# An attention and expert-FFN kernel on one core: the order of the first loads, a load issued from ScalarE's queue, and a planner that holds less urgent steps back

## The chip, the cores and the metric

The kernel runs on one core of a Trainium2 chip. A core has TensorE (PE, the matmuls, with its weight loads listed apart as PEld), VectorE (DVE), ScalarE (ACT), GpSimd (POOL) and SyncE (SP), which issues most of the DMA transfers. Each engine works through its own list of instructions in order and waits on semaphores for the others. The time is the device time of one launch in microseconds (us); before the change the median of three runs is 1022.4 us (1019.82 to 1022.9).

## The reference

x has 8 sequences of 1024 tokens with 256 features. A normalized attention without softmax over tokens, and a gated sum over 16 experts, each with a layer norm behind it:

```python
qkv = x @ Wqkv + bqkv;  q, k, v = split(qkv)          # each 256 wide
q = q - mean(q);  k = k - mean(k)
q2 = q*q / (sum(q*q) + eps);  q2 = q2 / norm of q2 along features
k2 = k*k / (sum(k*k) + eps);  k2 = k2 / norm of k2 along the tokens
kv = k2^T v;  t2 = q2 kv / sqrt(1024)                  # per sequence
x = layernorm(x + (v + t2) @ Wln + bln)
sel = sigmoid(x . expert_sel)                          # 16 gates per token
out = sum over e of sel_e * relu(x @ keys_e) @ values_e   # 256 -> 128 -> 256
x = layernorm(x + out)
```

## The kernel before, in words

Tokens are cut into 16 chunks of 512 (`NCHK`, two to a sequence). A matmul's operands are split into a high and a low part of fp32r type (`xh`/`xl` and so on), and three products are added (`passes3`, line 52). `nh`/`nl` are the same tokens with the tokens on the partitions, from x; `xh`/`xl` have the features there, from xT.

For each chunk c: `tokens_x` and `tokens_n` load and split x; `u_k` projects K (`kp`), squares it (`k`, sums in `ks`), scales it, splits it (`k2h`, `k2l`) and multiplies it with x's rows (`ap`, summed over a sequence in `asb`); `u_m` makes a matrix per sequence from it (`mc`, `pm`, `mh`, `ml`); `u_q` projects Q (`qp`), normalizes it (`qs`, `qj`, `qn`, `qy`) and turns it (`qt`, `q2h`, `q2l`); `u_y` makes the first layer norm's input (`yp`; `ych`, `ycl`, squares `ysq`) and the gates. For chunk 0 the gates go through `gates_first` (line 782): `tt`, `zt`, small steps on `gv`, `gy`, `zs`, `za`, a turn `gt`, a copy `gs`, and matmuls `gsp` that spread the first three gates over the partitions (`selb`). Then come 16 experts: `h` (or, for half of the pairs from chunk 1 on, `hx` and `hy` with fewer products), gating, the split `sh`/`sl`, and the second product into `w`. `u_end` normalizes and stores. `u_weights` loads and splits the experts' weights in four groups (`kst`, `keyh`, `keyl`; `vst`, `vst_m`, `valh`, `vall`). At the start K's weights (`sk`), Q's (`sq`), the output weights (`sl`) and V's (`svT`), a row of biases (`brow`) and small columns (`bc`, `eft`) are loaded; `brow` less its mean becomes `bhl` (lines 1231 to 1242), which is added to K and Q of chunks 0 and 1 by a matmul with `rows`.

No instruction stands where the code names it. `add` only records a task: its engine or engines, a cost, a key and what it reads and writes. `order` (line 202) then simulates all engines with these costs and writes the instructions out in the order in which its simulation starts them; a lower key goes first among the ready ones. Tiles share slots by tag (`SB_SLOTS`, `PS_SLOTS`); a task starts only when there is a slot for each new tile. Two features matter here:

- The first three second products of chunk 0 are goals (line 1125). Tasks on which a goal depends have a `tail`, the time from their start to the goal; they are the urgent ones. `sharpen` (line 183) simulates these alone with `pack`, 24 rounds forward and backward, and takes the start times of the best round as keys. All others have no tail, and their keys are the given ones.
- As long as an urgent task is left (`first`) and PE has nothing to start, `order` puts in a filler, `keep_warm` (line 433): two 128 by 128 matmuls into the tile `warm`, which show as four in the trace, with a planned 0.44 us. The number of fillers is fixed when the program is written, so PE runs them all, however fast they go.

The simulation's DMA (lines 285 to 290) gives a load 0.5 us of SP's queue, and then the transfers one behind the other. ACT's first instruction is the load of its function table (line 419).

```python
265  if e == "T" and self.idle and issued and first and now > 0.4:
266      fill = Task()
267      fill.eng, fill.fn, fill.news, fill.start, fill.done = e, {e: self.idle}, [], now, now + 0.44
```

Of the kernel before, what the change touches and what calls it, by code (L numbers as in the profile page):

```python
# [15 lines left out]
P = 128  # L16
# [10 lines left out]
WARM = 14  # L27
WINDOW = 10.47
# [69 lines left out]
class Task:  # L98
    __slots__ = ("eng", "cost", "key", "fn", "port", "deps", "outs", "bufs", "news", "start", "done", "n", "id", "tail")


class Work:
# [5 lines left out]
    def __init__(self, slots):  # L108
        self.slots, self.tasks, self.bufs, self.goals, self.idle = slots, [], [], {}, None
# [6 lines left out]
    def add(self, eng, cost, key, fn, r=(), w=(), port=False, after=()):  # L116

        t = Task()
        if len(eng) == 1:
            cost, fn, port = {eng: cost}, {eng: fn}, {eng: port}  # L120
        t.eng, t.cost, t.key, t.fn, t.port = eng, cost, key, fn, port
        t.id, t.deps, t.outs, t.bufs, t.news = len(self.tasks), set(after), [], {}, []
        for many, writes in ((r, False), (w, True)):
            for x in many:
                b, part = x if isinstance(x, tuple) else (x, None)
                for other, opart, owrites in b.accesses:
                    if (writes or owrites) and meet(part, opart) and other is not t:
                        t.deps.add(other)
                b.accesses.append((t, part, writes))
                t.bufs[b] = None  # L130
        for d in t.deps:
            d.outs.append(t)
        self.tasks.append(t)
        return t

    def pack(self, part, before, rank, release):
# [11 lines left out]
        while len(start) < len(part):  # L148
            now = heapq.heappop(events)
            moved = True  # L150
            while moved:
                moved = False
                for e in free:
# [20 lines left out]
                    end[t] = free[e] + (2.2 if e == "D" else 0.2 if e == "T" else self.LATENCY)  # L174
# [8 lines left out]
    def sharpen(self, rounds=24):  # L183

        part = [t for t in self.tasks if t.tail is not None]
        inside = set(part)
        deps = {t: [d for d in t.deps if d in inside] for t in part}
        outs = {t: [o for o in t.outs if o in inside] for t in part}
        late = max(-x for x in self.goals.values())
        release = {t: late + x for t, x in self.goals.items()}  # L190
        rank, best = {t: t.tail for t in part}, None
        for _ in range(rounds):
            start = self.pack(part, deps, rank, {})
            span = max(start[t] + x for t, x in self.goals.items())
            if best is None or span < best[0]:
                best = span, start
            back = self.pack(part, outs, start, release)
            rank = {t: back[t] + min(t.cost.values()) for t in part}
        for t in part:
            t.key = best[1][t] - 2000  # L200

    def order(self):
# [24 lines left out]
        while left:  # L227
# [7 lines left out]
            while moved:  # L235
# [5 lines left out]
                for e in free:  # L241
# [3 lines left out]
                    for entry in ready[e]:  # L245
# [7 lines left out]
                        if e == "G" and first and t.tail is None and t.port[e]:  # L253
                            continue
                        if e == "G" and t.port[e] and any(o.eng == "V" and o.port["V"] and k < key and w < now + 0.5 for k, _, o, w in ready["V"]):
                            continue
# [7 lines left out]
                    if best is None:  # L264
                        if e == "T" and self.idle and issued and first and now > 0.4:
                            fill = Task()
                            fill.eng, fill.fn, fill.news, fill.start, fill.done = e, {e: self.idle}, [], now, now + 0.44
                            fill.cost, fill.key, fill.bufs, fill.tail = {e: 0.44}, 0, {}, None
                            issued.append(fill)
                            free[e] = now + 0.44  # L270
                            heapq.heappush(events, free[e])
                        continue
# [12 lines left out]
                    if e == "D":  # L285
                        free[e] = now + 0.5
                        dma = max(dma, now + 1.3) + t.cost[e]
                        t.done = max(dma + 0.7, now + 2.2)
# [8 lines left out]
                    t.done += self.LATENCY  # L297
# [25 lines left out]
def attn_ffn_kernel(ctx, tc, x, xT, wqT, wk, wvT, wlnT, bcols, brows, selT, keys, values, outT):  # L323
# [55 lines left out]
    def high(key, h, b, n, r, w, free=True):  # L379

        if free:
            add("VS", {"V": c_dve(n, fast=True), "S": c_act(n, plain=True)}, key,
                {"V": lambda: V.tensor_copy(h(), b()), "S": lambda: S.copy(h(), b())}, r=r, w=w, port={"V": True, "S": False})
        else:
            add("S", c_act(n, plain=True), key, lambda: S.copy(h(), b()), r=r, w=w)
# [33 lines left out]
    S.preload_act_table_set("natural_log_exp_and_others")  # L419

# [16 lines left out]
    add("T", 0.44, -800, keep_warm, r=[ones], w=[warm])  # L437
    work.idle = keep_warm


    def stage(key, src, name, tag="sh"):
        b = sbuf(tag, [P, 2, D], name)
        add("D", 1.05, key, lambda: nc.sync.dma_start(out=b.ap, in_=src), w=[b])
        return b
# [51 lines left out]
    xh, xl, nh, nl = {}, {}, {}, {}  # L496
# [5 lines left out]
    def tokens_x(c, key):  # L502
        xh[c], xl[c] = h, l = [sbuf(t, [P, 2, CH], f"{t}{c}", FR) for t in ("xh", "xl")]
        if c == 0:
            b = sbuf("g3", [P, 2, CH], f"xf{c}")
            for i in range(2):
                w = slice(i * CH // 2, (i + 1) * CH // 2)
                add("D", 1.05, key, lambda w=w: nc.sync.dma_start(out=b[:, :, w], in_=xTv[:, :, w]), w=[(b, i)])
# [8 lines left out]
    def split(c, key, name, src, h, l, width):  # L517

        rows = h.shape[1]
        n = 1 if c < 2 else 2  # L520
        for i in range(n):
# [3 lines left out]
            add("D", 2.1 / n, key, lambda b=b, s=s: nc.sync.dma_start(out=b.ap, in_=src(s)), w=[b])  # L525
            high(key + 1.2, lambda s=s: h[:, s], lambda b=b: b.ap, 2 * CH // n, [b], [(h, part)], c < 2)
# [16 lines left out]
    def project(c, g, t, wh, wl, bias=None):  # L543
        for j in range(2):
# [4 lines left out]
            if bias is not None:  # L549
                terms += [(rows[:, bias, :], bhl[:, 0])]  # L550
            mm_group(t[:, j * D : (j + 1) * D], terms)
# [16 lines left out]
    def u_k(c, key):  # L568
# [7 lines left out]
        for g in range(2):  # L576
            tt = slice(2 * g, 2 * g + 2)
            t = psum(f"kp{c}_{g}", "h" if c == 0 else "att")
            if c < 2:
                add("T", c_mm(D, 14), key + g, lambda g=g, t=t: project(c, g, t, wkh, wkl, 1),  # L580
                    r=x_parts(c, g) + [wkh, wkl, rows, bhl], w=[t])
                squares(key + g + 0.7, q, g, s, t)
                continue
# [6 lines left out]
        for g in range(2):  # L590
# [3 lines left out]
            high(key + 3.5 + g * 0.3, lambda tt=tt: h[:, tt, :], lambda tt=tt: q[:, tt, :], CH, [(q, tt)], [(h, g)], c < 2)  # L594
# [109 lines left out]
    def u_q(c, key):  # L704
# [3 lines left out]
        for g in range(2):  # L708
            tt = slice(2 * g, 2 * g + 2)
            t = psum(f"qp{c}_{g}", "h" if c == 0 else "att")  # L710
            if c < 2:
                add("T", c_mm(D, 14), key + g, lambda g=g, t=t: project(c, g, t, wqh, wql, 0),
                    r=x_parts(c, g) + [wqh, wql, rows, bhl], w=[t])
                squares(key + g + 0.7, q, g, s, t)
                continue
# [34 lines left out]
        for ct in range(2):  # L750
# [6 lines left out]
            add("T", c_mm(P, 4), key + 6.5 + ct * 0.2, turn, r=[q, ident], w=[o])  # L757
# [457 lines left out]
    tokens_x(1, -110)  # L1215
    add("D", 0.1, -198, lambda: nc.sync.dma_start(out=bc.ap, in_=bcols), w=[bc])
# [10 lines left out]
    brow, mb = sbuf("sl", [P, 1, D], "brow"), tiny("brow_m")  # L1227
    bhl, rows0, rows = cbuf("bhl", [P, 1, D], FR), sbuf("t2", [P, 2, P], "rows0"), cbuf("rows", [P, 2, P], FR)
    add("D", 0.15, -197, lambda: nc.sync.dma_start(out=brow[:, 0], in_=brows), w=[brow])
# [123 lines left out]
    with tc.manual_schedule():  # L1353
        for t in work.order():
# [35 lines left out]
```

## Time and profile before

| | us |
|---|---|
| runs | 1019.82, 1022.4, 1022.9 (median 1022.4) |
| the profiled execution's own time | 1020.05 |
| its span, first to last instruction | 1018.3 |
| PE busy | 1008.1 (99%) |
| DVE busy | 784.8 (77%) |
| ACT busy | 667.1 (66%) |
| POOL busy | 470.5 (46%) |
| first K matmul of chunk 0 starts | 9.18 |
| first second product `w` starts | 63.96 |

A line of the profile has start and length in us, the engine, the line of the kernel, the operation, and the output and inputs by the program's names without numbers; "x12" is a number of instructions, and brackets hold the idle time of the engine before the instruction and what ended it. The chain of waits is followed back from the last instruction; the pieces of it lie end to end. A table by stretches has for each stretch the busy time of PE, PEld, DVE, ACT and POOL with the number of instructions, then the mean share of full speed at which TensorE's clock ran, the DMA engines' busy share, and GB/s.

### The profile page before, as it was taken

Reading aid. Unit: us, or ns where it says so; the run is one execution under the profiler, and the core shown is the slowest. Engines: PE = TensorE matmul, PEld = TensorE weight load, DVE = VectorE, ACT = ScalarE, POOL = GpSimd, SP = SyncE. Lnnn points to the kernel's source line nnn. Section 1 sums busy time; section 2 is a strip of 40 time slices with the busy share of each in tenths; the row PEclk is TensorE's granted clock in tenths of the full one; section 3 lists DMA queues with packets and bytes.
Section 4 is the critical chain, followed back from the end, with each engine's and each line's share of the span. In section 5 each row is a group of like instructions: output and inputs, shape, how many; then the busy total and the mean of one; then the engine's idle time right before and its main releaser. Section 6 shows DMA issues by size and latency. Waiting matters only on the chain.

```text
span 1018.3 us, 16317 instructions
## 1 busy us (share of the span) xinstructions
PE 1008.1 (99%) x5757; PEld 874.3 (86%) x5757; DVE 784.8 (77%) x1363; ACT 667.1 (66%) x1497; POOL 470.5 (46%) x424
## 2 busy tenths in 40 slices
PE   9999999999999999999999999999999999999996
PEld 9978879888898988889888888988889888888885
DVE  7889888687776887768787687867878687686775
ACT  7767566675676757766676676757666675665543
POOL 1001585546564464655536574454654536233430
PEclk9999999999999999999999999999999999999999
DMA  6144323233232323323223231323323222223131
GB/s 202 44 135 125 116 94 125 93 90 101 82 121 68 115 94 104 93 89 103 93 89 108 87 115 63 115 94 103 105 71 109 93 85 83 83 85 104 64 125 42
DMA packets 65298, 99.52 MB, mean 98 GB/s; under 512 B 6336, under 2 KB 24896, under 8 KB 65216
## 3 DMA queue, kind: packets, MB, share of 16 engines
q1 hardware_dynamic: 65216, 98.48, 30.1%
q8 instruction: 45, 0.74, 0.3%
q14 instruction: 37, 0.30, 0.1%
HBM read 89.54 MB, written 8.91 MB: 97 GB/s over the span
## 4 chain that ended last, share of the span: by engine, by line
PE 93%; DVE 3%; POOL 2%; ACT 1%; DMA 1%; issue 1%; POOLq 0%; DVEq 0%; ACTq 0%; SPq 0%
PE w L1121 32%; PE h L358 17%; PE hx L1074 11%; PE yp L358 8%; PE qp L358 4%; PE hy L1074 4%; PE kp L358 4%; PE ap L358 4%; PE warm L435 1%; PE qt L755 1%; PE sp L358 1%; PE pm L358 1%; DMA ksr<-keys 1%; PE mc L358 1%; DVE sl L1041 0%
## 5 line engine op out<-in xcount | busy, mean ns | idle before, releaser
L1121 PE MATMUL w<-sh,valh 128*128 128x512 f32 x504 | 158.4, 395 | 0.0
L1121 PE MATMUL w<-sh,vall 128*128 128x512 f32 x504 | 158.0, 394 | 0.0
L1121 PE MATMUL w<-sl,valh 128*128 128x512 f32 x504 | 157.7, 394 | 0.0
L1039 DVE SCALAR_TENSOR_TENSOR h<-h,selb 128x512 f32<-128x512 f32 x136 | 93.9, 692 | 31.0 <-PE h L358 27.8
L1121 PEld LDWEIGHTS w<-sh,vall 128*128 128x128 f32 x504 | 95.0, 188 | 22.1
L1121 PEld LDWEIGHTS w<-sl,valh 128*128 128x128 f32 x504 | 94.6, 188 | 22.4
L1040 ACT CAST sh<-h 128x512 fp32r<-128x512 f32 x136 | 73.6, 589 | 59.6 <-PE w L1121 55.5
L358 PE MATMUL h<-ych,keyh 128*128 128x512 f32 x272 | 109.7, 403 | 0.0
L358 PE MATMUL h<-ycl,keyh 128*128 128x512 f32 x272 | 107.5, 395 | 0.0
L358 PE MATMUL h<-ych,keyl 128*128 128x512 f32 x272 | 107.0, 393 | 0.0
L1041 DVE TENSOR_TENSOR sl<-h,sh 128x512 fp32r<-128x512 f32 x136 | 87.8, 683 | 23.1 <-ACT sh L1040 23.0
L1121 PEld LDWEIGHTS w<-sh,valh 128*128 128x128 f32 x504 | 86.2, 188 | 10.9
L389 POOL TENSOR_TENSOR k<-k,ks 128x512 f32<-128x512 f32 x25 | 30.9, 1257 | 101.9 <-DVE ks L566 101.9
L1093 DVE TENSOR_TENSOR hx<-hx,p 128x512 f32<-128x512 f32 x60 | 41.8, 696 | 29.8 <-ACT hy L1090 29.6
L1135 POOL TENSOR_TENSOR w<-w,ycl 128x512 f32<-128x512 f32 x30 | 38.2, 1296 | 55.5 <-DVE w L1132 55.5
L389 POOL TENSOR_TENSOR ysq<-ysq 128x512 f32<-128x512 f32 x15 | 20.1, 1338 | 91.1 <-ACT ysq L875 91.1
L358 PEld LDWEIGHTS h<-ych,keyl 128*128 128x128 f32 x272 | 51.1, 188 | 12.0
L358 PEld LDWEIGHTS h<-ycl,keyh 128*128 128x128 f32 x272 | 51.3, 189 | 10.5
L358 PEld LDWEIGHTS h<-ych,keyh 128*128 128x128 f32 x272 | 51.1, 188 | 10.7
L877 DVE SCALAR_TENSOR_TENSOR ycl<-yp,by,ych 128x512 fp32r<-128x512 f32 x32 | 24.0, 750 | 42.9 <-ACT ysq L875 42.9
L1090 ACT COPY hy<-hx 128x256 f32<-128x256 f32 x60 | 21.4, 357 | 46.9 <-PE hx L1074 45.4
L389 POOL TENSOR_TENSOR q<-q,qy 128x512 f32<-128x512 f32 x27 | 28.1, 1060 | 51.3 <-ACT sh L1040 43.7
(505 smaller groups left out, 3193.6 us busy)
## 6 DMA issues: line engine op xcount, KB each, us to landing
selb<-sel SPq DMA_DIRECT2D x253, 256.0 KB, 3.5
xf<-xT SPq DMA_DIRECT2D x30, 256.0 KB, 3.3
outT<-w SPq DMA_DIRECT2D x15, 512.0 KB, 3.0
nf<-x SPq DMA_DIRECT2D x28, 256.0 KB, 4.6
kst<-keys SPq DMA_DIRECT2D x6, 256.0 KB, 3.3
vst<-values SPq DMA_DIRECT2D x6, 256.0 KB, 3.7
nf<-x SPq DMA_DIRECT2D x2, 512.0 KB, 7.9
ksr<-keys SPq DMA_DIRECT2D x4, 256.0 KB, 3.5
```

What stands on the lines that cost most here:

```text
L358: T.matmul(out, w, r, start=first and i == 0, stop=last and i == len(terms) - 1)
L389: fns = {e: (lambda e=e: ENG[e].tensor_tensor(out(), a(), b(), op)) for e in engines}
L435: T.matmul(warm[:, :P], ones.ap, ones.ap, start=True, stop=True)
L877: add("V", c_dve(CH, ptr=True), k0 + 0.9, lambda t=t, jt=jt: V.scalar_tensor_tensor(yl[:, jt, :], t.ap, by[:, jt : jt + 1], f(yh[:, jt, :] ...
L1039: add("V", c_dve(CH), key + 0.1, lambda: V.scalar_tensor_tensor(at(t.ap), at(h.ap), 0.0, out(sel), ALU.max, ALU.mult), r=[h] + reads(sel), ...
L1040: add("S", c_act(CH, plain=True), key + 0.1, lambda: S.copy(out(a), at(t.ap)), r=[t], w=reads(a))
L1041: add("V", c_dve(CH), key + 0.1, lambda: V.tensor_tensor(out(b), at(t.ap), f(out(a)), ALU.subtract), r=[t] + reads(a), w=reads(b))
L1074: T.matmul(out(), wi, ri, start=first and i == 0, stop=True, skip_group_check=True)
L1090: add("S", c_act(n, plain=True), key + 0.07, lambda: S.copy(y1(), x1()), r=[x], w=[y])
L1093: add("V", c_dve(CH), key + 0.09, lambda: V.tensor_tensor(halves_(x.ap), halves_(x.ap), p5.ap.to_broadcast([P, 2, n]), ALU.add), r=[x, p5] ...
L1121: T.matmul(wps[c][v].ap, w[:, e % 4, v * P : (v + 1) * P], r[:, i], start=e == 0 and j == 0, stop=e == NE - 1 and j == 2)
L1135: add("G", c_pool(CH), key + 0.5, lambda v=v: G.tensor_tensor(w[:, v, :], w[:, v, :], f(ycl[c][:, v, :]), ALU.add), r=[(w, v), ycl[c]], w= ...
```

## The change

It has these parts:

- The first half of chunk 0's x is issued from ACT's DMA queue, and the table load becomes a task behind it; the second half stays on SP's queue.
- The big loads of the start get their order from a list, `LOADS`: K's weights, x of chunk 0 (second half), x of chunk 1, the bias row, rows of x of chunk 0, Q's weights, rows of x of chunk 1, output weights, V's weights. Before, the bias row was second.
- For chunks 0 and 1 the bias of K and Q is a task of its own behind the 12 matmuls of the projection.
- `sharpen` goes on for 110 tries in which ranks of the best order are scattered at random.
- In `order` a task that is not urgent is not begun while an urgent one, ready for the same engine, could start more than `GIVE` = 0.1 us before the end of it. This holds while urgent tasks are left.
- A filler has a planned 0.6 us before 6 us and 0.44 after; planned DMA costs become 1.24 times as large, with other fixed parts.
- For chunks from 2 on, the cast `nh` waits for the last K cast of the chunk before and for the turning of q two chunks back; the casts `nh` and `k2h` and the turning of q start only when there is also a slot for the low part (`hold`).

```diff
+GIVE = 0.1
+LOADS = ["sk", "xf0", "xf1_0", "brow", "nf0_0", "sq", "nf1_0", "sl", "svT"]
...
-    def sharpen(self, rounds=24):
+    def sharpen(self, rounds=24, tries=110):
...
+            rank.update((t, i - 9999.0) for i, t in enumerate(self.loads))
             start = self.pack(part, deps, rank, {})
             span = max(start[t] + x for t, x in self.goals.items())
...
+            if i < rounds:
+                back = self.pack(part, outs, start, release)
+                rank = {t: back[t] + min(t.cost.values()) for t in part}
+            else:
+                q = rnd.choice((0.02, 0.1, 0.4))
+                rank = {t: x + rnd.gauss(0, 3) if rnd.random() < q else x for t, x in best[2].items()}
         for t in part:
             t.key = best[1][t] - 2000
+        for i, t in enumerate(self.loads):
+            t.key = i - 3000.0
...
+                        if first and t.tail is None and any(o.tail is not None and w < now + t.cost[e] - GIVE for _, _, o, w in ready[e]):
+                            continue
...
-                        if e == "T" and self.idle and issued and first and now > 0.4:
-                            fill = Task()
-                            fill.eng, fill.fn, fill.news, fill.start, fill.done = e, {e: self.idle}, [], now, now + 0.44
+                        if e == "T" and self.idle and first and self.warm.start is not None:
+                            fill, cold = Task(), 0.6 if now < 6 else 0.44
+                            fill.eng, fill.fn, fill.news, fill.start, fill.done = e, {e: self.idle}, [], now, now + cold
...
-                        dma = max(dma, now + 1.3) + t.cost[e]
-                        t.done = max(dma + 0.7, now + 2.2)
+                        dma = max(dma, now + 1.6) + 1.24 * t.cost[e]
+                        t.done = dma
...
-    S.preload_act_table_set("natural_log_exp_and_others")
-
...
+    add("S", 1.3, -2150, lambda: S.preload_act_table_set("natural_log_exp_and_others"), w=[])
...
-            for i in range(2):
-                w = slice(i * CH // 2, (i + 1) * CH // 2)
-                add("D", 1.05, key, lambda w=w: nc.sync.dma_start(out=b[:, :, w], in_=xTv[:, :, w]), w=[(b, i)])
+            first, second = slice(0, CH // 2), slice(CH // 2, CH)
+            add("S", 0.5, -2200, lambda: nc.scalar.dma_start(out=b[:, :, first], in_=xTv[:, :, first]), w=[(b, 0)]).lag = 2.2
+            loads.append(add("D", 1.05, key, lambda: nc.sync.dma_start(out=b[:, :, second], in_=xTv[:, :, second]), w=[(b, 1)]))
...
+        in_turn = [turns[n] for n in (f"k{c - 1}", f"q{c - 2}") if n in turns]
...
+            high(key + 1.2, lambda s=s: h[:, s], lambda b=b: b.ap, 2 * CH // n, [b], [(h, part)], c < 2,
+                 in_turn if name == "nf" else (), (l,))
...
+    def add_bias(t, bias):
+        for j in range(2):
+            T.matmul(t[:, j * D : (j + 1) * D], rows[:, bias, :], bhl[:, 0], start=False, stop=True, skip_group_check=True)
...
-                add("T", c_mm(D, 14), key + g, lambda g=g, t=t: project(c, g, t, wkh, wkl, 1),
-                    r=x_parts(c, g) + [wkh, wkl, rows, bhl], w=[t])
+                add("T", c_mm(D, 12), key + g, lambda g=g, t=t: project(c, g, t, wkh, wkl, 1), r=x_parts(c, g) + [wkh, wkl], w=[t])
+                add("T", c_mm(D, 2), key + g, lambda t=t: add_bias(t, 1), r=[rows, bhl], w=[t])
...
+            turns[f"k{c}"] = high(key + 3.5 + g * 0.3, lambda tt=tt: h[:, tt, :], lambda tt=tt: q[:, tt, :], CH, [(q, tt)], [(h, g)], c < 2, hold=(l,))
...
+            turns[f"q{c}"] = add("T", c_mm(P, 4), key + 6.5 + ct * 0.2, turn, r=[q, ident], w=[o], hold=[q2h[c], q2l[c]])
```

## The prediction

> **What bounds the kernel now.** I read four views in this order: the busy times, TensorE's waits, the chain of waits with the timeline of the first 70 us, and a table by stretches. Busy times:
>
> ```profile
> PE 1008.1 (99%) x5757; PEld 874.3 (86%) x5757; DVE 784.8 (77%) x1363; ACT 667.1 (66%) x1497; POOL 470.5 (46%) x424
> ```
>
> TensorE (PE) is busy for 1008.1 of 1018.3 us, and its list of waits holds 2.0 us in all: 1.1 before its first instruction and 0.9 once, near 151 us. So after the start-up nothing but fewer or faster matmuls can help. But "busy" counts filler too. The chain of waits in the first 70 us (start, us, what) shows it:
>
> ```profile
> 1.06 8.37 PE warm L435 x60
> 9.43 6.61 PE kp L358 x56
> ...
> 33.32 0.44 PE warm L435 x4
> ...
> 40.49 2.23 PE warm L435 x20
> ...
> 60.06 0.64 PE warm L435 x4
> ...
> 61.75 2.56 PE warm L435 x12
> 64.31 1.98 PE w L1121 x6
> ```
>
> `warm` writes a tile that nobody reads; 8.37 + 0.44 + 2.23 + 0.64 + 2.56 = 14.2 us of it. The kernel's time is TensorE's work plus this filler plus the tail, so the change can win only out of those 14.2 us, and can lose by adding to them. What ends the first 8.37 us is on the timeline (start, us, instruction, in brackets the idle time before it):
>
> ```profile
> 0.81 0.43 SPq L443 DMA_DIRECT2D sk<-wk  x1
> 1.29 0.46 SPq L1229 DMA_DIRECT2D brow<-brows  x1
> 1.80 0.94 SPq L508 DMA_DIRECT2D xf<-xT  x2
> ...
> 3.67 0.69 DVE L465 TENSOR_REDUCE sk_m<-sk 128x2 f32<-128x512 f32 x1 [1.13 <-DMA sk<-wk]
> ...
> 5.96 0.62 ACT L383 CAST xh<-xf 128x512 fp32r<-128x512 f32 x1 [0.85 <-DMA xf<-xT]
> 6.48 0.50 ACT L1238 ACTIVATE bhl<-brow,brow_m 128x256 fp32r<-128x256 f32 x1
> ...
> 7.72 0.48 DVE L1241 SCALAR_TENSOR_TENSOR bhl<-brow,brow_m,bhl 33x256 fp32r<-33x256 f32 x1
> ```
>
> The K weights (sk) are there at 3.67, the first half of x only at 5.96; the bias row is the last piece, finished at 8.20. The fillers, written into PE's list beforehand, run on to 9.18. Last, the stretches (PE, PEld, DVE, ACT, POOL busy, PE clock, DMA):
>
> ```profile
> 16.00:40.00 24.00, 24.00 (x172) 22.68 (x171) 22.56 (x59) 19.31 (x52) 0.16 (x1) 1.00 0.10 36
> 44.00:62.00 18.00, 18.00 (x105) 14.19 (x104) 14.47 (x39) 16.54 (x44) 0.00 (x0) 1.00 0.38 115
> 60.00:80.00 20.00, 20.00 (x95) 16.38 (x95) 17.23 (x34) 11.88 (x27) 0.00 (x0) 0.91 0.47 145
> 80.00:100.00 20.00, 20.00 (x111) 17.26 (x110) 18.94 (x34) 15.56 (x33) 4.46 (x4) 1.00 0.51 146
> ```
>
> From 16 to 40 us VectorE (DVE) works 22.56 of 24 us: it is the second bound there. From 44 to 62 the chain of the gates runs through small steps, and ScalarE (ACT) is at 92%.
>
> **The change part by part.** I count against the profiled execution (1020.05 us; span 1018.3, so 1.75 lie around it). The median of the three runs is 1022.4, 2.35 above it; the sum is a difference, and I take it off the median.
>
> *1. Loads.* The first half of x is issued on ACT at about 0.8. One issue takes 0.43 to 0.46 us on SP's queue, and I take that for ACT. Behind it on ACT stand the table load (1.28), the cast of one_r and that of rows; ACT then sat idle 1.90 us before 4.60, so 0.45 more is hidden; without that idle time it would cost 0.45. SP's queue loses this half and, before xf1, brow: its second half of x is issued 1.0 us earlier, xf1 1.0 earlier, brow 1.0 later. Arrival of the half: not under sk's own 2.8 us from issue (3.6), not above 5.96 less 1.0 for the earlier issue and 0.4 for the 128 KB of brow at the 327 GB/s of the stretch from 5 to 10 us (4.6). I take 4.3, nearer to the row of the same tile. Two queues at once the trace does not show; sk may lose between 0 and 0.8 (256 KB at that rate), I take 0.4: 4.1. From sk to wkh it was 0.93 us (3.67 to 4.60). Then DVE has half of wkh 0.34, wkl 0.48 twice and xl 0.69: 2.0, less little overlap, and the first K matmul is ready at 6.9 instead of starting at 9.18: **-2.3** (-3.0 to -1.5).
>
> The Trainium skill, "DMA: Bandwidth & Descriptors", section "Issuing engines are not separate DMA queues", speaks against this: queues of several engines run on the same 16 DMA engines, and a second one saves only the time of issuing. By that rule the half would come near 5.0, and the term would be about -1.6 in place of -2.3; no run here shows two queues yet.
>
> *2. The bias after the product.* 12 matmuls start without bhl, two for the bias follow. Same matmuls, same time each (0.118 us apart). But brow now comes after xf1's 512 KB.
>
> *3. The hole behind it.* xf1 was cast at 9.25, its xl done at 11.61: 2.36 later. Issued 1.0 earlier with brow gone, it arrives between 7.8 and 9.25; I take 8.6, so chunk 1's K product is ready at 10.95. Chunk 0's 24 matmuls end at 6.9 + 2.8 = 9.7. Unless the bias fills it (4 x 0.118 = 0.47, if bhl is there), **+0.9** (0 to +1.3) comes back as filler.
>
> *4. Where it goes next.* The squares of K read the product with its bias, so they start after brow: about 10.9, four of 0.48 + 0.20 = 2.7, sums at 13.7 where the trace has 14.31. From there DVE is nearly full until 40 us, so only 0.6 of the 1.4 won arrives; **+0.8** (0 to +1.4) turns up as filler near 33 or 40 us.
>
> *5. A better order.* The planner tries 110 more orders, scattered at random, for the urgent steps. It can win at most DVE's idle 1.44 us of 16 to 40 and part of the 3.5 of 44 to 62; it can lose where its model errs. I take DVE's idle time up to 40 us nearly whole, as that is the row it is nearest to: **-1.2** (-3.0 to +1.0).
>
> *6. Less urgent steps held back.* Near 41 us q2l waits for two copies (bqbc, bkbc) that nobody needs yet: 0.35. In the gates' chain, each from the end of the one step to the start of the next: Ln behind qj 0.7, Exp behind the copies of yv0s 1.0, two steps behind q's newton 0.35, turning gt behind kp 0.35, gsp behind h 0.6, selb behind k's squares 0.2. That is 3.55 in all, of which I take two thirds, -2.4. But three steps that PE did there (qp 1.68, kp 1.37, h 1.39 = 4.4 us) are useful work; where one is held back, PE runs filler and does it later. I let one of them go: +1.5. Net **-0.9** (-3.5 to +2.0).
>
> *7. The end of the start-up.* sl is ready at 62.33, w starts at 63.96: the fillers between were planned at 0.44 and ran at half clock:
>
> ```profile
> 62.00:64.00 2.00, 2.00 (x13) 2.00 (x11) 2.00 (x5) 1.95 (x4) 0.00 (x0) 0.51 0.56 174
> ```
>
> Of these 1.6 us I take **-0.7** (-1.6 to 0), a little under half: the change re-prices fillers only before 6 us, but the steps that they stand between will lie differently. The Trainium skill, "TensorE: Matmul & The Clock Gate", Part 1, gives half rate after an idle window of some 3.4 us; here PE was never idle from 58 to 62, but ran matmuls of 16 rows, so the measurement decides; by the page's rule alone there would be no slow window, and the term would be the whole -1.6.
>
> *8. The steady part.* Casting x's rows (nh) must now wait for the K cast before it and for the turning of q two chunks back. In the trace nh is cast at 179.3, q is turned at 193.0: it moves 14 us back on ACT, and with it nl (2.55 us) on POOL. Its reader, ap, starts at 232.8: 37 us of slack. Behind the waiting nh on ACT stand others' casts, but these are ordered by the same plan. I cost it at 0; if the slack were gone, each of 14 chunks could pay up to the 0.9 us that hx once waited, +12.6; the low end is 0, as PE waits for nothing there.
>
> Sum: -2.3 + 0.9 + 0.8 - 1.2 - 0.9 - 0.7 = **-3.4 us**; 1022.4 - 3.4 = 1019.0 (from the profiled execution: 1016.65).
>
> **Rivals.**
> *A: hidden.* VectorE's full stretch swallows terms 1 to 5 and the filler merely moves from 1 to 9 us to 33 to 60. For it: 22.56 of 24, and brow comes late. Against: DVE itself idles 3.8 us between 5 and 14. Only the 0.35 at 41 us and term 7 win: about -1.0: 1021.4.
> *B: slower, VectorE in debt.* The rule holds back on DVE what it did between 40 and 62 for later: xl 1.28, nl 1.36, keyl 2.05, vst_m 1.37, q 1.28, k 0.69, vall 1.35 = 9.4 us. From 60 to 100 DVE has 2.77 + 1.06 = 3.8 free. Beyond 3.8 us put off, weights and gates come late and PE waits. All of it: +5.6, less 2.5 for the terms that stay (1 to 5: -1.8, 7: -0.7): +3.1: 1025.5, more where the gates themselves come late. Against: DVE had 3.5 idle in 44 to 62, where small steps still fit.
> *C: the order hardly changes* (the loads arrive as before, by bytes alone): 1022.4.
>
> **How the numbers follow.** Forecast 0.44, A 0.26, C 0.08, B 0.22. A difference of 0.3% (3.07 us) is about what a measurement of this kernel can tell from no change. The forecast's own case lies beyond it: faster 0.44; A and C within: 0.34; B slower: 0.22. The forecast's own range is 1015 to 1019.3. The range over all reaches from 1014.5 (terms 5 and 6 at their good ends) to 1025.5, which leaves out most of B's far half and a little below: under 0.2.
>
> **What would show it.** Right: kp begins near 7, not 9.2; a short filler before chunk 1's K product; the first w near 59 to 61; the sum of warm near 10 to 11. Term 1 falls if xh of the first half is cast after 5; term 6 if filler between 44 and 62 grows more than w comes forward. B would show as PE waits between 62 and 100; term 8 as ap waiting for nl in every chunk. I am wrong altogether if PE waits appear after 160 us.

## The result and the profile after

The kernel after the change takes 1028.9 us (median of four runs, 1027.86 to 1030.58), the kernel before 1021.11 in the same comparison (1019.24 to 1022.9): a ratio of 1.0077, 95% interval 1.0059 to 1.0096. It is slower by 7.8 us, where I had forecast 3.4 us faster, and lies above the upper end of my range, 1025.5. One thing is needed to read the numbers below: runs of one and the same kernel differ by up to 4.5 us with the mean clock of their records (in three of the comparisons the kernel before took 1018.95 to 1020.11 us at 0.997, and 1022.27 to 1023.55 at 0.994 to 0.995), so I compare ratios, and places within the traces.

The profiled execution of after took 1027.97 us (span 1026.2, mean clock 0.997). Its busy times:

```profile
PE 1011.5 (99%) x5765; PEld 878.1 (86%) x5765; DVE 783.3 (76%) x1367; ACT 667.1 (65%) x1499; POOL 471.1 (46%) x419
```

PE is busy for 3.4 us more, of which 1.2 is filler, and the span is 7.9 us longer. The difference shows better in PE's list of waits (line and tile, released by what; us in all, times, longest):

```profile
PE hx L1099 <- ACT p L1109: 3.5, 5, 0.7
PE warm L449 <- POOL ones L437: 1.1, 1, 1.1
PE qp L572 <- DVE q L742: 0.8, 1, 0.8
PE ap L375 <- DVE k2l L405: 0.7, 2, 0.4
```

Before, hx waited once for 0.9 us; now it does five times, and two more waits are new. "I am wrong altogether if PE waits appear after 160 us" has come true. To see when the time is lost, I take the first second product `w` of each chunk in both traces:

| first w of chunk | before, us | after less before, us |
|---|---|---|
| 0 | 63.96 | -0.39 |
| 1 | 133.9 | +1.65 |
| 2 | 195.2 | +1.03 |
| 13 | 865.5 | +8.39 |
| last w | 1007.7 | +8.25 |

So the start-up neither won nor lost much (+1.03 at chunk 2), and the steady part loses 7.36 us between chunks 2 and 13. In that stretch PE runs the same 3830 matmuls; the gaps behind `sp` grew by 3.65 us, those of `hx` by 1.27, `kp` 1.13, `ap` 0.93 and `wv` 0.60.

The chain of waits of after at the start (start, us, what):

```profile
1.06 7.05 PE warm L449 x36
8.11 2.85 PE kp L572 x24
10.96 1.34 PE warm L449 x12
12.30 1.42 PE kp L572 x12
13.72 0.48 PE kp L576 x4
...
62.15 1.59 PE h L375 x6
63.73 1.40 PE w L1146 x6
```

The first product is earlier, as meant, and fillers follow it. The bias matmuls (L576) come only behind chunk 1's product. Up to the first w the list holds 108 fillers (14.77 us) against 100 (13.56), and 12 matmuls fewer: chunk 2's first K product (1.37 us), which before stood at 54.95, has gone behind the first w.

What the loads did, on the timeline of after:

```profile
0.80 0.49 ACTq L525 DMA_DIRECT2D xf<-xT  x1
...
3.24 1.28 ACT L453 ACT_TABLE_LOAD   x1
4.50 0.69 DVE L483 TENSOR_REDUCE sk_m<-sk 128x2 f32<-128x512 f32 x1 [1.95 <-DMA sk<-wk]
4.81 0.62 ACT L400 CAST xh<-xf 128x512 fp32r<-128x512 f32 x1 [0.28 <-DMA xf<-xT]
```

sk lands at 4.50 instead of 3.67, the half of x at 4.81 instead of 5.96.

Now one place of the steady loss: PE's gap between `sp` and `hx`, 1.10 us from start to start at 274.2 (again near 398, 521, 644 and 767), where before has 0.29. PE in after, then in before:

```profile
274.22 0.40 PE L375 MATMUL sp<-ycl,ewt 128*128 128x512 f32 x1
275.32 0.39 PE L1099 MATMUL hx<-th,ksh 128*128 128x256 f32 x1 [0.70 <-ACT p L1109]
```

```profile
272.90 0.40 PE L358 MATMUL sp<-ycl,ewt 128*128 128x512 f32 x1
273.19 0.38 PE L1074 MATMUL hx<-th,ksh 128*128 128x256 f32 x1
```

ACT in after, then in before:

```profile
271.86 0.73 ACT L1170 ACTIVATE wy<-wy,c_zero 128x512 f32<-128x512 f32 x1 [2.01 <-DVE wy L1168]
272.62 0.72 ACT L1171 ACTIVATE wy<-wy,c_zero 128x512 f32<-128x512 f32 x1
273.37 1.25 ACT L796 COPY yv4s<-ysq 64x512 f32<-64x512 f32 x2
274.53 0.36 ACT L1108 COPY hy<-hx 128x256 f32<-128x256 f32 x1
```

```profile
268.43 0.72 ACT L1145 ACTIVATE wy<-wy,c_zero 128x512 f32<-128x512 f32 x1
...
270.49 1.25 ACT L771 COPY yv4s<-ysq 64x512 f32<-64x512 f32 x2 [0.58 <-POOL ysq L389]
272.40 0.36 ACT L1083 COPY hy<-hx 128x256 f32<-128x256 f32 x1 [0.67 <-PE hx L1074]
```

Before, ACT waited for PE at the copy of hx (0.67); after, the copy starts as soon as ACT gets to it, and PE waits. Three steps stand ahead of it, and the first had waited 2.01 us for VectorE. Further up on POOL, after and before:

```profile
258.84 2.75 POOL L405 TENSOR_TENSOR nl<-nf,nh 128x512 fp32r<-128x512 f32 x2
261.55 1.48 POOL L405 TENSOR_TENSOR wsq<-wsq 128x512 f32<-128x512 f32 x1
```

```profile
242.27 1.30 POOL L389 TENSOR_TENSOR nl<-nf,nh 128x512 fp32r<-128x512 f32 x1
...
258.41 1.57 POOL L389 TENSOR_TENSOR wsq<-wsq 128x512 f32<-128x512 f32 x1 [1.51 <-ACT wsq L1137]
```

nl, which POOL did in a gap near 240 us, now stands right ahead of the sum wsq that ends a chunk. That is where the added wait has moved it.

### The profile page after: what moved, and what is told of

Its sections match the earlier page's. It is cut to its first block, busy times and chain, and to the rows that moved or that the text cites. A ratio compares the mean times of both kernels' runs of the same rounds, so it can differ in the third digit from the quotient of the medians.

```text
span 1026.2 us, 16323 instructions
## 1 busy us (share of the span) xinstructions
PE 1011.5 (99%) x5765; PEld 878.1 (86%) x5765; DVE 783.3 (76%) x1367; ACT 667.1 (65%) x1499; POOL 471.1 (46%) x419
## 4 chain that ended last, share of the span: by engine, by line
PE 70%; DVE 9%; POOL 8%; ACT 7%; issue 6%; DMA 0%; POOLq 0%; SPq 0%; DVEq 0%; ACTq 0%
PE w L1146 25%; PE h L375 10%; PE hx L1099 9%; PE hy L1099 4%; PE kp L572 4%; PE qp L572 4%; PE yp L375 4%; PE ap L375 3%; POOL nl L405 1%; PE warm L449 1%; POOL xl L405 1%; POOL w L1160 1%; PE pm L375 1%; DVE h L1064 1%; POOL q L405 1%
## 5 line engine op out<-in xcount | busy, mean ns | idle before, releaser
L405 POOL TENSOR_TENSOR kss<-kss 128x512 f32<-128x512 f32 (+1 forms) x19 | 23.7, 1249 | 62.4 <-ACT kss L622 62.4
L583 ACT ACTIVATE q<-q,c_zero 128x256 f32<-128x256 f32 x56 | 28.1, 502 | 34.3 <-DVE q L742 34.3
```

The source lines that it names most:

```text
L405: fns = {e: (lambda e=e: ENG[e].tensor_tensor(out(), a(), b(), op)) for e in engines}
L583: S.activation(q[:, t, :], q[:, t, :] if src is None else src[:, t % 2 * D : (t % 2 + 1) * D], AF.Square, bias=c_zero.ap, accum_out=s[:, t ...
```

## The experiments

**e1: the wait for the turn kept to the start.** Theory T says that the wait costs the steady part.

```
-                 in_turn if name == "nf" else (), (l,))
+                 in_turn if name == "nf" and c < 4 else (), (l,))
```

> The changed kernel, but the casts nh wait for the K cast and the turning of q only for chunks 2 and 3; from chunk 4 on this wait is gone. Theory T (this wait, of no use after the start-up, puts nh and nl late in every chunk): the 6.7 us that the changed kernel loses between the first w of chunk 1 (135.6 against 133.9) and of chunk 13 (873.9 against 865.5) are gone, and part of the 2.0 lost before: 1020 to 1022 us. Rival S (the steady part suffers from the other edits of the planner, its DMA prices, the slots held for low parts, or the start-up's shift): it stays at 1027 to 1030.

Measured: 1024.01 us (ratio to before 1.0038, 1.0024 to 1.0052). From chunk 2 to 13 it loses 0.77 us instead of 7.36. PE's waits:

```profile
PE qp L572 <- DVE q L742: 1.6, 1, 1.6
PE warm L449 <- POOL ones L437: 1.1, 1, 1.1
```

All waits of hx are gone. The one for q that is left lies at 117 us, in chunk 1. The time is still 2 us above theory T's upper end: what remains is the start-up, 3.68 us at chunk 2, where after lost 1.03. Up to the first w PE's list is the same in both, matmul for matmul; e1's trace has two stretches there in which TensorE ran at half rate, after's has none and that of before one (last section). By an estimate from these records (1.7 us for a stretch, and 0.92 us for the full rate that begins later in after, by the start of its first product), the start-up loses some 2 us in both when the clock is that of before.

**e2: the wait for the turn alone, added to the kernel before**, with nothing else of the change (and no `hold`).

> The kernel before with one edit of the change alone: nh of chunks from 2 on waits for the last K cast of the chunk before and for the turning of q two chunks back. Theory T: 6 to 8 us slower than before, 1027 to 1029, and hx stalls about 1.1 us once in every second chunk, as in the changed kernel. Rival S: within 1.5 us of before.

Measured: 1028.13 us, ratio 1.0082 (1.0057 to 1.0106); the start is that of before to 0.03 us up to chunk 1, then 7.17 us are lost between chunks 2 and 13. The same five waits as in after:

```profile
PE hx L1078 <- ACT p L1088: 3.5, 5, 0.7
```

e1 and e2 together show the cause of the steady loss from both sides: this one line. That any new plan would lose as much is ruled out: e1 keeps `hold` in every chunk and is planned anew, as are e4 to e8 below, and they lose 0.3 to 1.4 us between chunks 2 and 13. Why the line costs is asked of e3, e13 and e15.

**e3: the late nl given to VectorE** from chunk 4 on, all of the change kept.

```
-  ... "V" if c < 2 else spare(key))
+  ... "V" if c < 2 or name == "nf" and c >= 4 else spare(key))
```

> The changed kernel with its wait, but from chunk 4 on nl is computed on VectorE and not on POOL. T1 (the wait costs because nl, 2.55 us on POOL, now stands ahead of wsq, xl and ysq, so that the copies of yv come late on ACT, ahead of the copies of hx): 4 to 7 us faster than the changed kernel, 1022 to 1025. T2 (the late nh cast on ACT or the slots are what costs): no faster than 1 us, or slower by VectorE's extra 1.3 us a chunk.

Measured: 1033.92 us, ratio 1.0138 (1.0123 to 1.0153); hx now waits 6.4 us in eleven places. A miss for T1. It is slower, as T2 allows, but the plan is a new one, so this doesn't tell whether POOL was the place.

**e13: nl put behind wsq in POOL's list** from chunk 4 on, by moving the instructions after the plan was made, so that PE, VectorE and ACT keep their order; in SyncE's list the loads that take over nl's buffers move with it.

```
-            nl<-nf,nh x2
             wsq<-wsq
+            nl<-nf,nh x2
```

> The changed kernel with its wait for the turn in every chunk, and one swap in POOL's list from chunk 4 on: the two nl (2.75 us) go behind the sum wsq of the chunk's end instead of ahead of it; loads that take over nl's buffers go with them. All else stays where it was. Theory Q (what the wait costs is POOL: the later nl stands ahead of wsq, so all that follows on POOL and ACT, with hx's copies at the end of it, comes late): PE's waits of hx for p (3.5 us in five chunks) shrink to less than 1.5, and 2 to 5 us come off the 1028.9 of the changed kernel: 1024 to 1027. Rival A (ACT: the cast nh stands at another place among ACT's steps and that is what delays): no change, 1028 to 1029.5. Rival V (the steady loss is spread over DVE's full list): no change either, and the waits stay.

Measured: 1034.69 us, ratio 1.0138 (1.0116 to 1.016); 9.98 us lost between chunks 2 and 13, and the five waits of hx are as they were, 3.5 us. POOL and ACT at the same place:

```profile
263.45 1.30 POOL L405 TENSOR_TENSOR wsq<-wsq 128x512 f32<-128x512 f32 x1 [1.17 <-ACT wsq L1162]
264.71 2.54 POOL L405 TENSOR_TENSOR nl<-nf,nh 128x512 fp32r<-128x512 f32 x2
```

```profile
275.25 0.73 ACT L1170 ACTIVATE wy<-wy,c_zero 128x512 f32<-128x512 f32 x1 [2.01 <-DVE wy L1168]
```

This trace runs 3.39 us behind that of after here. wsq is 1.49 us earlier by that measure, but ACT's wy waits the same 2.01 us: in between, ACT's cast of wv stands behind ych and ysq, which wait for PE's `yp`, and VectorE's wy behind a step that waits for the next ysq. Against before, the order on PE and VectorE has changed too. After, then before:

```profile
269.77 0.40 PE L375 MATMUL wv<-wv2hl,one_r 128*128 128x512 f32 x1
269.88 0.75 DVE L902 SCALAR_TENSOR_TENSOR ycl<-yp,by,ych 128x512 fp32r<-128x512 f32 x1 [1.97 <-ACT ysq L900]
270.55 0.69 DVE L1064 SCALAR_TENSOR_TENSOR h<-h,selb 128x512 f32<-128x512 f32 x1
271.15 0.68 DVE L1168 SCALAR_TENSOR_TENSOR wy<-v,wv 128x512 f32<-128x512 f32 x1
```

```profile
267.07 0.40 PE L358 MATMUL wv<-wv2hl,one_r 128*128 128x512 f32 x1
267.51 0.69 DVE L1143 SCALAR_TENSOR_TENSOR wy<-v,wv 128x512 f32<-128x512 f32 x1 [0.89 <-PE wv L358]
268.57 0.75 DVE L877 SCALAR_TENSOR_TENSOR ycl<-yp,by,ych 128x512 fp32r<-128x512 f32 x1 [0.38 <-ACT ysq L875]
```

Before, PE's wv follows `yp` at once and VectorE's wy goes ahead of the second ycl; after, wv stands behind six h matmuls and wy behind that ycl and an h. e13 keeps these lists, so an earlier wsq on POOL can't bring wy forward. Theory Q falls: POOL's order alone isn't the place. That the plan laid out the other lists so because nl is late on POOL is my reading; no run shows it. The swap also costs something of its own: PE now waits 2.9 us, in six places, for POOL's low parts of wv and yv, and of the 5.9 us that its last w comes behind that of after, 3.3 lie ahead of chunk 2, where this trace has two stretches at half rate and after's none.

**e15: in ACT's list, hx's two copies ahead of those of yv**, in chunks 4, 6, 8, 10 and 12; again everything else as in after.

```
             ACTIVATE wy x2
-            COPY yv4s<-ysq x2
             COPY hy<-hx
             COPY p<-hx
+            COPY yv4s<-ysq x2
```

> The changed kernel with one swap in ACT's list in chunks 4, 6, 8, 10 and 12, five places in all: the two copies of yv (1.25 us) go behind the copies of hx to hy and p instead of ahead of them. Theory L (the plan's order on ACT: hx's product ends near 273.7, ACT comes to its copies at 274.53 since wy and the two yv copies stand ahead of them, wy itself having waited 2.01 us for VectorE; POOL alone was shown not to be it): the five waits of hx for p (3.5 us in all) go, the gaps between sp and hx fall from 1.10 to below 0.5 us, and up to 4 us come off where the clock is equal: 1025 to 1027 against 1028.9. Rival Y (the delay is upstream, in wv and wy, and moves to the next reader, yv's sum on POOL): the waits of hx go, yv waits come, and the time stays at 1028 to 1030.

Measured: 1028.0 us, ratio 1.0058 (1.0038 to 1.0078). ACT there:

```profile
273.08 0.72 ACT L1171 ACTIVATE wy<-wy,c_zero 128x512 f32<-128x512 f32 x1
274.19 0.36 ACT L1108 COPY hy<-hx 128x256 f32<-128x256 f32 x1 [0.39 <-PE hx L1099]
```

ACT waits for PE again, all five waits of hx are gone, and the gaps behind sp are 4.35 us less in all; the loss between chunks 2 and 13 falls from 7.36 to 4.78. Theory L is right for the five waits, but 1.8 us of the 4.35 come back in small gaps (kp 0.52 more than in after, hy 0.54, hx 0.42, w 0.24). The time is the one that rival Y gave, but the waits for yv that it expected are not there, so what takes the 1.8 us back is open. By the times alone e15 can't be told from after, as their intervals overlap; the gain is read from the places within the traces.

**e4 to e8: parts of the start-up.** On e1's kernel as the base: e4 loads the bias row second, e5 drops the rule with `GIVE`, e6 has no tries, e7 issues the first half of x from SyncE again. e8 is the kernel before with only the new DMA price. All five get a new plan.

```
e4  -LOADS = ["sk", "xf0", "xf1_0", "brow", ...
    +LOADS = ["sk", "brow", "xf0", "xf1_0", ...
e5  -if first and t.tail is None and any(... now + t.cost[e] - GIVE ...): continue
e6  +tries=0
e7  -add("S", 0.5, -2200, lambda: nc.scalar.dma_start(...)).lag = 2.2
    +loads.append(add("D", 1.05, key, lambda: nc.sync.dma_start(...)))
e8  +dma = max(dma, now + 1.6) + 1.24 * t.cost[e]; t.done = dma
```

> As e1, and the bias row is loaded second again. If the late bias row is what eats the start-up's gain (the squares of K wait for it), the first w comes 1 to 2 us earlier than in e1 and the time is 1 to 2 us less, 1019 to 1021. If VectorE or the clock sets the start-up, the first w stays within 0.5 us of e1's.

> The changed kernel with its wait for the turn kept to chunks 2 and 3 (the base, 1024.01 us) and less the rule that holds less urgent steps back. Its list has the 24 K matmuls of chunk 2 ahead of the first second product, the base has none, the kernel before 12. Theory P (put off): the rule brings the first second product forward only by moving such work behind it, 12 K matmuls (1.64 us) and VectorE's steps that later make PE wait 1.78 us at 117 us for q. Then the first w comes later than the base's 65.2 by up to 2 us, the wait at 117 is gone, and the first w of chunk 1 comes at 136.5 or earlier (base 138.6): 1021 to 1022.5 us. Rival S (the bias that lands late, with K's squares starting at 13.99 us): the loss is in the first 16 us and stays: 1023.5 to 1025. Rival K (clock): the base has one half-rate window of 3.4 us more than the kernel before, 1.7 us; then the time follows the number of such windows in the profile, not the order.

> The same base less the 110 tries. Its list has 12 K matmuls of chunk 2 ahead of the first second product, as in the kernel before, and 12 fillers' groups there against 8. Theory P: the tries too only moved work over that line; the first w comes 0 to 1.5 us later than 65.2, but chunk 1's first w not later than 138: 1022.5 to 1024 us. The prediction's term 5 (the tries win 1.2 us): 1025.2. Rival S: no change, 1024.

> The same base with the first half of x issued from SyncE's queue again, the table load still a task. The half lands near 5.5 instead of 4.8. The prediction's term 1 (the earlier x is worth 1.3 to 2.3 us): first K matmul over 1 us later than 8.1 at the same clock, and 1025.3 to 1026.3 us. Theory P (what the first product waits for doesn't count, since the squares wait for the bias and VectorE is full to 40 us): no more than 0.5 later, 1023.5 to 1024.5 us; with 12 K matmuls of chunk 2 again ahead of the first w, down to 1022.5.

> The kernel before with nothing but the new planned cost of a DMA transfer (1.24 times, other fixed parts). The loads keep their order but the steps between them are planned later, with 9 groups of fillers ahead of the first second product against 5. If the planner's order by better prices is worth something: 1018 to 1019.5 us. Theory P holds nothing back here: 12 K matmuls of chunk 2 stay ahead of the first w, no wait at 117, so 1019.5 to 1021.5 us. If more planned fillers are what costs: 1022 to 1024.

| run | us | ratio to before, interval | first w, us | fillers, us |
|---|---|---|---|---|
| e1 (base) | 1024.01 | 1.0038, 1.0024 to 1.0052 | 65.19 | 13.85 |
| e4 bias row second | 1027.63 | 1.0072, 1.0048 to 1.0096 | 69.17 | 18.50 |
| e5 no GIVE | 1029.68 | 1.0078, 1.0061 to 1.0095 | 76.30 | 22.15 |
| e6 no tries | 1028.32 | 1.0068, 1.0049 to 1.0087 | 71.93 | 19.85 |
| e7 x from SyncE | 1029.89 | 1.0084, 1.0063 to 1.0104 | 75.18 | 21.52 |
| e8 before, new price | 1028.19 | 1.0057, 1.0037 to 1.0078 | 71.44 | 17.19 |

All five expectations missed, on the same side: each run is slower than any case I had written down. e8's third case, that more planned fillers cost, had the direction. Against the base, taking any one part out or back costs 0.30 to 0.46%, 3 to 5 us (the intervals of e4 and e6 just touch that of e1), and the price alone costs the kernel before 5.8; most of it goes into fillers. My theory P had put chunk 2's K product at the centre. In e5 it is back, the wait at 117 is gone, and 1.6 us come back between chunks 0 and 1, but 8.3 us more of filler swamp this. The parts don't add up: each comes with a new plan of the start.

**e9: the load alone, without a new plan.** Base as before; the plan is made as in e1, then the first half of x is issued from SyncE behind sk.

```
-nc.scalar.dma_start(out=b[:, :, first], in_=xTv[:, :, first])
+nc.sync.dma_start(out=b[:, :, first], in_=xTv[:, :, first])   (moved behind sk)
```

> The base of before (the changed kernel, wait for the turn in chunks 2 and 3 only: 1024.01 us), every instruction in the same place on PE, DVE, ACT and POOL; only the first half of x is issued from SyncE's queue behind sk, so SyncE's later loads go 0.5 us later. This prices the load alone, without a new order. Theory R (rigid list): PE has no wait in the first 60 us, its list of products and fillers runs through, so an earlier operand is worth nothing and a later one costs in full once the fillers ahead of it run out. The half lands 0.7 to 1.2 us later than 4.81; K is then ready 0.7 to 1.2 after the fillers' end (6.95 in the base's profile): a PE wait of that length at 7 us and 0.3 to 1.2 us on the time: 1024.3 to 1025.2. The prediction's term 1 (the load is worth 2.3 in time): 1026.3. The 5.9 us that the same edit cost with a new order (1029.89) would then be the order's, not the load's.

Measured: 1024.24 us, ratio 1.003 (1.0017 to 1.0044), the same as e1 within the intervals. Where x landed, on ACT:

```profile
4.37 0.62 ACT L400 CAST xh<-xf 128x512 fp32r<-128x512 f32 x1 [0.36 <-DMA xf<-xT]
...
7.23 0.62 ACT L400 CAST xh<-xf 128x512 fp32r<-128x512 f32 x1 [1.43 <-DMA xf<-xT]
```

From SyncE the first half came at 4.37, earlier than from ACT's queue (4.81 in after, 4.91 in e1), and sk at 3.71 instead of 4.50; the second half and the loads behind it are later. The wait that I expected at 7 us is not there: what the first product needs was ready at 6.50. The second half's xl was ready at 8.57, and PE came to it at 9.3, since TensorE's full rate began only at 6.98 here (4.98 in e1) and the fillers ended near 7.9 instead of 6.95; with e1's clock it would have come near 8.4, by estimate, and waited 0.2 us. So the 1.15 us from 5.96 to 4.81 come from the bias row's place in the order, not from the second queue. Theory R's first half stands: PE's list has no wait here, and the first half, earlier by 0.4 to 0.5 us, changes nothing in the time. What an operand costs that comes behind the end of the fillers is not shown.

**e10 and e11: without the later fillers.** e10 is the base with the 18 groups behind the first 9 left out after planning; e11 also puts chunk 0's four bias matmuls (L576) from behind chunk 1's first K product to ahead of it.

```
+        n += t.fn[t.eng] is keep_warm
+        if t.fn[t.eng] is keep_warm and n > 9:
+            continue
```

> The same base with the 18 groups of fillers behind the first K product left out (72 matmuls, 8.4 us; the 9 groups ahead of it stay); nothing else moves. Theory R: the fillers stand where the plan expects a wait, and the wait on the chip is shorter: part of the 8.4 us is pure loss, and PE waits show for the rest. Win of 1 to 5 us: 1019 to 1023. Rival W (the waits are real): as much PE wait as filler was, 1023.5 to 1024.5. Rival K (clock): idle PE loses its full clock for windows of 3.4 us, and each costs 1.7 us: 1025 to 1029.

> The run with the fillers left out, and PE's four bias matmuls of chunk 0 put ahead of chunk 1's K product instead of behind it (bhl was ready at 9.82, the bias matmuls ran at 13.72, K's squares at 13.99). If the late bias costs (term 4 taken as a cost of PE's order): squares start near 10.5 to 11, VectorE's sums 2.5 us earlier, first w 0.5 to 2.5 us before that of the run without fillers, and the time 0.5 to 2.5 less. If VectorE or the gates' chain is what later waits are for: within 0.5 us of it.

Measured: e10 1022.09 us, ratio 1.0 (0.9986 to 1.0014), 0.38% under the base; e11 1021.81, ratio 0.9996 (0.9982 to 1.0009). PE's longest waits in e10:

```profile
PE pm L375 <- DVE q2l L784: 1.5, 1, 1.5
PE qp L572 <- DVE q L742: 1.1, 1, 1.1
```

Some 2 to 4 us of the fillers were pure loss (2.15 by the middle values of e9 and e10, which are of one comparison and differ on PE in these fillers alone; 3.9 by the ratios of e1 and e10), and of the 4.5 us that PE does wait behind the first filler, 3.1 are for VectorE. In e11 K's squares begin at 11.15 instead of 12.43, and the time doesn't follow (0.28 us, with overlapping intervals): the late bias is not what costs.

**e12 and e14: the same for the kernel before.** e12 leaves out its 10 later groups; e14 also keeps only 12 of the first 15. In the edit above, 9 becomes 15 and 12.

> The kernel before with its 10 groups of fillers behind the first K product left out (40 matmuls, 5.4 us in its profile), nothing else changed. Theory R: PE waits for part of it only: 1 to 3.5 us less than the kernel before, and the first w near 61 to 63 instead of 63.96. Rival W: same time with waits in place of fillers. Rival K: idle PE falls to half rate, 1 to 4 us more.

> The kernel before with 12 groups of fillers at the start instead of 15, and none behind them. Its first K product needs the bias row's last piece at 8.20 us, while 15 groups ended at 9.18 in the profile and at 10.14 in the run that left only the later ones out. Theory R: the list is rigid, so the start comes forward by what ended later than the operands: 0.9 to 1.9 us, and 1018 to 1019.2 against 1020.0 of that run. Rival D (VectorE, 34 of 40 us from 10 to 50, takes it back): 1020, no change. Rival K: fewer fillers move the clock's full rate later, and it is 1020 to 1022.

Measured: e12 1020.0 us, ratio 0.9979 (0.9968 to 0.9991); e14 1017.96, ratio 0.9973 (0.9957 to 0.9989), its first w at 61.54. Both beat both kernels; e14's middle value is the best of the study, though its interval overlaps that of e12. Neither needs anything of the change.

## Why the prediction was wrong

The step that failed is **term 8**: "37 us of slack ... I cost it at 0". The slack of nl's reader was there: ap waits in two places only, 0.7 us, and that for k2l. But I had looked only at the moved task's reader. The steps that stand behind its new place have no such slack: wsq, wv and wy end a chunk, and the next hx's copies stand behind wy and yv's copies in ACT's list. I even wrote "Behind the waiting nh on ACT stand others' casts, but these are ordered by the same plan", which doesn't mean ordered well. My own upper bound, 14 chunks by 0.9, took hx's wait as the unit; 7.36 us came, of it 3.65 behind sp. Five waits of hx are explained (e15); some 4.8 us in gaps of at most 0.53 us are shown to come from the wait for the turn (e1, e2), but not from which step. That stays open.

A second step failed by being left out: **the new planned prices of the DMA have no term in the sum**, so they stood at 0 without a reason. Alone, they cost the kernel before 5.8 us (e8). The start, forecast at -3.4, came out at +1.03 at chunk 2 in this trace and +3.68 in e1's, so it would have missed without term 8 too.

Point by point for the rest:
- **Term 1 (-2.3).** wkl was done at 6.94, as I said (6.9), but by two errors that cancel: sk came at 4.50, not 4.1, and from there it took 2.44 us, not 2.8. The product began at 7.87, since 36 fillers stood ahead of it in the list and ran at half rate until 6.9 (0.213 us apart, then 0.112): 1.31 won. In e1, with the same list, the full rate began at 4.98 and the product at 6.95, 2.23 earlier than before. So which of the two a profile shows is the clock's doing. My 4.3 for the half was 4.81. The Trainium skill, "DMA: Bandwidth & Descriptors", section "Issuing engines are not separate DMA queues", which I had weighed and not followed, has queues of several engines share the same DMA engines; the estimate that I made from it, 5.0, is nearer to the measured 4.81 than mine. e9 agrees that the transfers share: with the half on a queue of its own, sk landed 0.8 us later.
- **Terms 2 and 3 (0, +0.9).** The hole before chunk 1's product is 1.34 us of filler, at the upper end of my 0 to 1.3.
- **Term 4 (+0.8).** Squares at 13.99 instead of 10.9: the bias row's last piece was ready at 9.82, but PE's list had the bias matmuls behind chunk 1's product. e11 shows no cost of it in the end, in the kernel without the later fillers.
- **Terms 5 and 6 (-1.2, -0.9).** Taken out alone (e6, e5) the tries cost about 3 us and the rule about 4, so they do more than I gave them; but all the parts of the start together bring back only some 2 of the 5.8 us that the new prices cost (e8 against e1), and no run has them with the old prices. I had summed them on top of the order of before, which the same change had taken away. The "PE step put off" was real: kp, 1.37 us before, went behind the first w. PE's wait of 0.8 us at 115 in chunk 1 is new too; in e5, with the rule gone, it is not there.
- **Term 7 (-0.7).** No slow clock, and no filler directly ahead of the first w, in after. The clock was luck and not the planner's doing: e1, with the same list, has a slow stretch from 63.01 to 66.42.
- **Rival B** (VectorE in debt) has its wait, for q at 115 us rather than between 60 and 100, and 0.8 us of it. It wasn't the cause.

The start sums up: -0.39 at the first w; then +1.64 for kp, +0.94 in ap with the wait for q, -0.81 as w no longer runs in a slow window, +0.27 of small gaps: +1.65 at chunk 1.

## What to carry to other kernels

A wait that protects the start must not act in every pass: e2 pays 7.2 us for one that was meant for the start. Before costing a moved task at nothing, look not only at its reader but at who stands behind its new place on each engine, and what they have to spare. Where an in-order list holds fillers, count PE's waits first: with none, an earlier load brings nothing forward until fillers ahead of its reader are taken out, and taking out some (e14) may be the whole gain.

## What the runs showed of the hardware

**Half rate with PE busy.** PE is busy throughout these rows of e1 and yet runs at half rate for part of them (columns as in the prediction):

```profile
54.00:58.00 4.00, 4.00 (x15) 3.19 (x14) 3.64 (x10) 3.06 (x9) 0.00 (x0) 0.73 0.22 64
58.00:62.00 4.00, 4.00 (x21) 2.49 (x20) 1.00 (x4) 2.20 (x7) 0.00 (x0) 1.00 0.48 141
...
64.00:66.00 2.00, 2.00 (x6) 1.58 (x5) 1.94 (x4) 2.00 (x7) 0.00 (x0) 0.50 0.16 54
```

In the clock records of the 17 traces there are 24 such stretches ahead of the program's last 10 us. They last 3.41 us or twice that and fall between 50 and 78 us, the later ones where the first w is late: one in before (62.06 to 65.47), two in e1, none in after. In the 3.41 us ahead of each of the 24 PE ran matmuls of one column (tt), of 48 (zt) or of 16 rows (gsp); in the stretches themselves it mostly ran h, w and fillers. A stretch of 3.41 us costs about 1.7. How many there are differs even between traces with the same list: up to the first w PE's is the same in after (none), e1 (two) and e9 (one of 6.83 us). The full rate, too, begins anywhere from 4.03 to 6.98 us in the 17 traces, though the fillers always start at 1.06. So a place in the start-up of one profile can move by 1 to 3 us without any change of the kernel. The Trainium skill, "TensorE: Matmul & The Clock Gate", Part 1, says that such windows of some 3.4 us run free and that an idle one brings half rate. The length agrees; but here PE was busy by the profile, for 3.14 to 3.41 us of the 3.41 ahead of each stretch (ends of matmuls are modelled there), and in e10, where it waited for 2.96 us between 10 and 50 us, the clock stayed at 1.00 in that stretch. That small matmuls count as idle would fit; it was not tried by itself.

**A second table load.** With the load as a task of the plan, ACT loaded its table twice, at 1.33 and 3.24 us, 1.28 us each: the casts of one_r and rows were put ahead of the task, and a load came in front of them. It is hidden, since ACT had nothing else to do before 4.81.
